# Moving 48 checks of the adjacency matrix from layers 2 and 3 of a graph network into the pair loop of layer 1

## The chip, the cores and the metric

The kernel runs on one core of a Trainium2 chip. The metric is device time in microseconds (us), from the start to the end of the program on that core. A core has five engines that run side by side, each with its own queue of instructions: TensorE (PE in the profile; its weight loads are PEld), VectorE (DVE), ScalarE (ACT), GpSimd (POOL) and SyncE (SP). In this kernel SP only issues transfers (DMAs); POOL issues a few too.

## What is computed

Four graph layers in a row, on 4096 nodes with 64 features each, with one and the same 4096 x 4096 adjacency matrix `adj` (about 0.8% of its entries are 1, the diagonal is all 1). Each layer is applied to `h = max(layernorm(x), 0)` and its result is added to `x`:

```python
# layer 0: graph attention, 8 heads and an output head, softmax over the edges
# layer 1: hyperbolic attention
adj_att = sigmoid(left[:, None] + right[None, :] + b_att) * adj
support_t = einsum('ij,ijd->id', adj_att, logmap(h_i, h_j))
out1 = proj(expmap(h, support_t))
# layer 2: mean over the neighbours
deg = clip(sum(adj, axis=1) + 1, 1, None)
z = concat([h, (adj @ h + h) / deg]) @ W + b
out2 = relu(z) / max(norm(relu(z)), 1e-12)
# layer 3: the last 100 edges of a row, with halving weights
rank = cumsum(adj != 0, axis=1); k = min(rank[:, -1:], 100)
w = (adj != 0) * where(pos > 0, 0.5 ** (k - pos), 0)     # pos = rank - (deg - k)
out3 = w @ (h @ weight) + bias
```

The fast path of the kernel stores edges as bytes and so is right only if every entry of `adj` is 0 or 1. The kernel therefore reads the whole matrix once more as floats and counts other values. If any is found, a slow general kernel is run after it. On the given inputs none is found.

## The kernel before, in words

**The check.** `count_odd` (line 951) is one check. It loads one tile `raw` of 128 x 2048 floats (1 MB, two buffers) through SP's queue and runs one VectorE instruction over it (line 955), which also sums into a column of `bad`. The matrix has 64 such tiles; the iterator `todo` (line 959) hands them out. Sixteen are done in layer 0's output attention (line 2107), the other 48 in layers 2 and 3.

**Layer 1, the pairs** (`pairs_fast`, from line 2230). The nodes are cut into 8 groups of 512, and a job is a pair of groups (gi, gj), gj <= gi: 36 jobs, 8 of them diagonal. The loop from line 2396 on is a software pipeline over n = -2 to 36. In one step n it works on four jobs: `done` (n-1), `now` (n), `soon` (n+1) and `later` (n+2), in four parts s = 0 to 3:

- `load_edges(later)`: one or two tiles `nm` of 256 KB by SP, four buffers.
- `score_pair(soon)` in each part: PE, then ACT (tile `sg`, line 2284).
- s = 0: `bring(done)`, which adds PE's sums `accj` to VT on DVE (lines 2382 to 2384).
- s = 0 and 2: `turn(now)`: PE transposes and two DVE multiplications (line 2332); not for diagonal jobs.
- s = 1 and 3: `sums(now)`, the large matmuls (line 2339).
- `distance(later)` in each part (PE, ACT) and `square(later)` in s = 1 and 3 (ACT; tile `sqy`, three buffers).
- s = 1: `factor(soon)`, two DVE instructions (line 2313); s = 3: `weigh(soon)`, two more (line 2320).

The loop stands in `with in_order()`: PE, ACT and DVE each keep exactly the written order. SP is not held by it. Outside such blocks a planner (list scheduler) orders each engine's instructions when the kernel is built.

**The finish of layer 1** (`finish_steps`, line 2429; `nodes`, line 2562) turns VT into new node values, a quarter of the nodes at a time, in a long chain of small DVE instructions with ACT between, and ends in the tile `HH` (in the profile `XAf`), which layer 2's matmuls read.

**Layer 2** (lines 2668 to 2719): for each half hf of the columns, PE multiplies `HH` with the edge bytes `m` (line 2679) in 8 steps q, and with `sel` for the degrees (line 2692). Then four groups go through `layer2_group`, a chain over PE, ACT and DVE that ends in the values `SS` for layer 3. In a step q with `hf or q > NQ // 2` a check is issued: 3 in the first half, 8 in the second. `issue_after` keeps them behind the finish.

**Layer 3** (lines 2724 to 2792): four units u of 1024 columns. For each of 32 blocks j: PE counts edges into `pv` (lines 2748, 2756), ACT turns counts into weights (line 2765), PE adds up (`sacc`, line 2730). The edges `m` come in 8 loads of 512 KB per unit (line 2741), with three buffers. Checks stand beside the blocks: 12 in u = 0, 9 in u = 1, 8 each in u = 2 and 3. All are tied by `issue_after(valued[-1])` to the last `layer2_group`'s values (line 2664), so none runs before that.

Of the kernel before, what the change touches and what calls it, by code (L numbers as in the profile page):

```python
# [18 lines left out]
ALU = mybir.AluOpType  # L19
# [7 lines left out]
NB = N // P  # L27
# [808 lines left out]
def kernel(  # L836
# [1392 lines left out]
    def pairs_fast(es, VT):  # L2229
# [19 lines left out]
        with ExitStack() as ss:  # L2249
# [129 lines left out]
            def bring(gi, gj):  # L2379
# [6 lines left out]
                for way in ways(gi, gj):  # L2386
                    del sig[way], edges[way]

            def job(n):
                return jobs[n] if 0 <= n < len(jobs) else None  # L2390

            load_edges(*jobs[0])
            with in_order():
                for n in range(-2, len(jobs) + 1):
                    done, now, soon, later = (job(n + k) for k in range(-1, 3))
                    if later and n + 2 > 0:
                        load_edges(*later)
                    for s in range(4):
                        if soon and s // 2 < len(ways(*soon)):
                            score_pair(*ways(*soon)[s // 2], s % 2 * 2)  # L2400
                        if s == 0 and done:
                            last_column(*done, 2)
                            bring(*done)
                        if s % 2 == 0 and now and now[0] != now[1]:
                            turn(*now, s)
                        if s % 2 and now:
                            sums(*now, s - 1)
                        if s == 2 and now:
                            last_column(*now, 0)
                        if later:  # L2410
                            distance(*later, s)
                            if s % 2:
                                square(*later, s - 1)
                        if s == 1 and soon:
                            factor(*soon)
                        if s == 3 and soon:
                            weigh(*soon)

    def finish_steps(bs, VQ, VT, fold_v, pabs, f, f2, kp, pf, ac2, wide, ps):

# [91 lines left out]
    def layers_fast(es, wide, *sums):  # L2512
# [41 lines left out]
            base=0,  # L2554
            channel_multiplier=1,
        )
        ready, valued = [], []

# [24 lines left out]
        def not_before_nodes():  # L2585
            return tc.issue_after(ready[-1].ins)
# [32 lines left out]
        def layer2_group(b0, part, deg):  # L2619

            bs = slice(b0, b0 + GB)
            hg = h[:, bs, :]
            pn = ps.tile([P, GB, D], F32, name="pnf", tag="misc")
            for b in range(GB):
                nc.tensor.matmul(
                    pn[:, b, :], lhsT=part[:, b * P : (b + 1) * P], rhs=fold_h, start=True, stop=True
                )
            cat = work.tile([P, GB, 2 * D], F32, name="cat", tag="cat")
            nc.gpsimd.tensor_copy(cat[:, :, 0:D], hg)
            nc.vector.scalar_tensor_tensor(cat[:, :, D:], pn, 1.0 / VALH, hg, ALU.mult, ALU.add)  # L2630
            nc.vector.tensor_tensor(cat[:, :, D:], cat[:, :, D:], over(deg, D), ALU.mult)
            cT = work.tile([P, G], F32, name="cT", tag="cT")
            transpose_to(cT, [cat[:, b, :] for b in range(GB)], P, ps, nc.scalar.copy)
            pz = ps.tile([P, GB, D], F32, name="pz", tag="misc")
            for b in range(GB):
                nc.tensor.matmul(
                    pz[:, b, :], lhsT=cT[:, b * P : (b + 1) * P], rhs=w2, start=True, stop=True
                )
            zt = work.tile([P, GB, D], F32, name="zt", tag="zt")
            nc.vector.tensor_tensor(zt, pz, b2t.unsqueeze(1).to_broadcast([P, GB, D]), ALU.add)  # L2640
            nc.scalar.activation(zt, zt, AF.Relu)
            sq = work.tile([P, GB, D], F32, name="sq2", tag="sq2")
            nc.scalar.activation(sq, zt, AF.Square)
            nrm = small("nrm", GB)
            nc.vector.tensor_reduce(nrm, sq, AX.X, ALU.add)
            nc.vector.tensor_scalar(nrm, nrm, 1e-24, None, ALU.max)
            nc.scalar.activation(nrm, nrm, AF.Sqrt)
            nc.vector.reciprocal(nrm, nrm)
            nc.vector.tensor_tensor(zt, zt, over(nrm, D), ALU.mult)
            xg = x[:, bs, :]  # L2650
            nc.vector.tensor_tensor(xg, xg, zt, ALU.add)

            for _ in norm_steps(bs, work, "sq2"):
                pass
            hT = work.tile([D, G], F32, name="hT3", tag="hT3")
            transpose_to(hT, [h[:, b, :] for b in range(b0, b0 + GB)], D, ps, nc.scalar.copy)
            pu = ps.tile([P, GB, D], F32, name="psup", tag="misc")
            for b in range(GB):
                nc.tensor.matmul(
                    pu[:, b, :], lhsT=hT[:, b * P : (b + 1) * P], rhs=w3, start=True, stop=True  # L2660
                )
            nc.scalar.copy(SS[:, bs, 0, :], pu)
            lo = work.tile([P, GB, D], F32, name="lo3", tag="lo3")
            valued.append(nc.vector.tensor_tensor(lo, pu, SS[:, bs, 0, :], ALU.subtract))
            nc.scalar.activation(SS[:, bs, 1, :], lo, AF.Copy, scale=LO)


        with tc.tile_pool(name="ps_nacc", bufs=6, space=PSUM) as ps_acc:
            for hf in range(2):
                accs = [ps_acc.tile([P, G], F32, name="nacc", tag="nacc") for _ in range(NS)]  # L2670
                dc = ps_acc.tile([P, G], F32, name="dc", tag="nacc")
                for q in range(NQ):
                    m = work.tile([P, JT, HW], U8, name="m2", tag="m2", bufs=3)
                    nc.sync.dma_start(m, mask_d[q][hf])
                    m8 = m.bitcast(F8)
                    for t in range(JT):
                        j = q * JT + t
                        for k in range(NS):
                            nc.tensor.matmul(  # L2679
                                accs[k],  # L2680
                                lhsT=HH[:, j].rearrange("p s d -> p (s d)"),
                                rhs=m8[:, t, k * G : (k + 1) * G],
                                start=(j == 0),
                                stop=(j == NB - 1),
                            )
                    if hf or q > NQ // 2:
                        with not_before_nodes():
                            count_odd(work, next(todo))
                    for t in range(JT):
                        j = q * JT + t  # L2690
                        for k in range(NS):
                            nc.tensor.matmul(
                                dc[k * O : (k + 1) * O, :],
                                lhsT=sel[:, j * O : (j + 1) * O],
                                rhs=m8[:, t, k * G : (k + 1) * G],
                                start=(j == 0),
                                stop=(j == NB - 1),
                            )
# [25 lines left out]
        for u in range(4):  # L2724
# [14 lines left out]
            for q in range(NQ):  # L2739
                m = work.tile([P, JT, HO2], U8, name="m3", tag="m3", bufs=3)  # L2740
                nc.sync.dma_start(m, mask_d[q][u // 2][:, :, hs])
                for t in range(JT):
                    j = q * JT + t

                    pv = ps_v.tile([P, HO2], F32, name="pv", tag="pv")
                    for k in range(NK):
                        r = ((u % 2) * NK + k) * O
                        nc.tensor.matmul(
                            pv[:, k * G : (k + 1) * G],
                            lhsT=blk[r : r + O, j, :],  # L2750
                            rhs=late[r : r + O, u // 2, :],
                            start=True,
                            stop=False,
                        )
                    for k in range(NK):
                        nc.tensor.matmul(  # L2756
                            pv[:, k * G : (k + 1) * G],
                            lhsT=tri,
                            rhs=m[:, t, k * G : (k + 1) * G].bitcast(F8),
                            start=False,  # L2760
                            stop=True,
                        )

                    w = work.tile([P, HO2], I16, name="w3b", tag="w3b", bufs=3)
                    nc.scalar.activation(w, pv, AF.Relu)  # L2765
                    if (j % 4 == 1 or j == 31 and u == 1) if u else j % 5 and j > NB // 2:
                        with tc.issue_after(valued[-1].ins):
                            count_odd(work, next(todo))
                    if last is not None:
                        add_up(*last)  # L2770
                    last = (j, w)
# [113 lines left out]
```

## Time and profile before

| | us |
|---|---|
| median of 3 runs | 2073.34 (2065.35 to 2073.9) |
| profiled execution, its own time | 2079.71 |
| its span, first to last instruction | 2077.9 |

| engine | busy us | share of the span | instructions |
|---|---|---|---|
| PE | 1830.8 | 88% | 19323 |
| PEld | 825.1 | 40% | 19340 |
| DVE | 1533.3 | 74% | 2239 |
| ACT | 1476.6 | 71% | 1439 |
| POOL | 86.0 | 4% | 125 |

Stages in the trace, in us from the start of the span: layer 0 to about 1200, the setting up of layer 1 to 1222, its pairs to about 1675, its finish beside the first matmuls of layer 2 to about 1747, layer 2 to about 1829, layer 3 (u = 0 beside the last groups of layer 2) to 2067, and the last outputs to 2078.

How to read the lines: a group's line gives source line, engine, operation, tile written <- tiles read, shape and count; then busy us in all and mean ns of one; then the engine's idle time before them and what ended it. In a timeline a line begins with the start and the length in us, and brackets hold the idle time just before. A line of waits has the total, the number and the longest wait. Matmul lengths are modelled. Shares of the whole span mix stages with different limits, so a stage's own stretch is what counts.

### The profile page before, as it was taken

The page shows a single profiled execution, that of the slowest core. Times are in us where ns is not written, and L with a number is a line of the kernel's source. Part 1 is how long each engine was busy: PE and PEld are TensorE (multiplying, and loading weights), DVE is VectorE, ACT ScalarE, POOL GpSimd, SP SyncE. Part 2 cuts the span into 40 slices and gives each one's busy share as a digit, 9 for nine tenths or more (in the row PEclk, how much of TensorE's full clock was granted, in tenths as well). Part 3 has the DMA queues.
Part 4 walks back from the last instruction along what each step waited for, and adds up shares of the span by engine and source line. Part 5 has one row for each costly group of instructions (what it writes and reads, how often), then busy time and mean ns, then how long its engine had stood idle before and what let it go on. Part 6 is the DMA issues. An engine that isn't in the chain of part 4 may idle for free.

```text
span 2077.9 us, 44185 instructions
## 1 busy us (share of the span) xinstructions
PE 1830.8 (88%) x19323; PEld 825.1 (40%) x19340; DVE 1533.3 (74%) x2239; ACT 1476.6 (71%) x1439; POOL 86.0 (4%) x125
## 2 busy tenths in 40 slices
PE   5889989999999999994898959999999968799777
PEld 3444444444444444442343523333333333443222
DVE  5779988998689889996889756656555687625554
ACT  3778988899689879984778757777777732257446
POOL 2000100100000000001011000000000000000000
PEclk8899999999999999996999959999999978979889
DMA  9946645345011101004875311111111045715885
GB/s 111 179 112 99 100 89 97 133 159 190 21 48 68 44 30 73 33 2 164 314 246 200 112 37 31 37 46 36 41 41 36 26 164 187 269 41 192 291 315 185
DMA packets 117015, 239.04 MB, mean 115 GB/s; under 512 B 11062, under 2 KB 84006, under 8 KB 102054
## 3 DMA queue, kind: packets, MB, share of 16 engines
q1 hardware_dynamic: 101996, 192.95, 27.0%
q0 software_dynamic: 14816, 43.18, 11.6%
q8 instruction: 153, 2.51, 0.5%
q14 instruction: 50, 0.41, 0.1%
HBM read 245.37 MB, written 49.46 MB: 142 GB/s over the span
## 4 chain that ended last, share of the span: by engine, by line
PE 34%; DVE 11%; issue 7%; ACT 5%; DMA 5%; POOL 0%; SPq 0%; POOLq 0%; DVEq 0%; ACTq 0%
PE accj L2339 9%; PE acco L2132 3%; PE pf L2329 2%; PE pl L2273 2%; DMA mo<-edges 2%; DMA raw<-in_adj_dram 2%; PE pu L2293 2%; PE accC L1541 2%; PE pl L2279 2%; DVE raw L955 2%; PE pu L2294 1%; PE accB L1541 1%; PE nacc L2679 1%; DVE B L1211 1%; PE pv L2756 1%
## 5 line engine op out<-in xcount | busy, mean ns | idle before, releaser
L1205 ACT ACTIVATE st<-srow,nt 128x2048 int8<-128x2048 f32 x352 | 682.8, 1994 | 78.2 <-DVE B L1211 77.3
L1211 DVE TENSOR_TENSOR B<-st,mres 128x1024 int32<-128x1024 int32 x256 | 312.0, 1221 | 69.5 <-PE accC L1541 44.5
L1541 PE MATMUL accB<-B,ybh 128*32 128x512 fp8e4 x3072 | 340.0, 385 | 13.3 <-DVE B L1211 13.3
L1541 PE MATMUL accD<-B,ybh 128*32 128x512 fp8e4 x2048 | 303.2, 388 | 23.6 <-DVE h L1657 23.6
L1541 PEld LDWEIGHTS <-ybh 128*32 128x32 bf16 (+1 forms) x6656 | 198.3, 98 | 236.4 <-issue 75.6
L1541 PE MATMUL accC<-mres,ych 128*32 128x512 fp8e4 x2272 | 268.3, 380 | 0.0
L1541 PE MATMUL accC<-B,ycn 128*32 128x512 fp8e4 x2272 | 268.1, 380 | 0.0
L1541 PE MATMUL accL<-B,ybh 128*32 128x512 fp8e4 x1536 | 221.4, 391 | 4.6 <-DVE h L1661 4.5
L1541 PEld LDWEIGHTS <-ych 128*32 128x32 f16 x4096 | 170.2, 99 | 114.8 <-issue 10.2
L1199 DVE TENSOR_SCALAR st<-srow,nt 128x2048 uint8<-128x2048 f32 x160 | 205.6, 1285 | 2.5
L2339 PE MATMUL accj<-sg,who 128*64 128x512 f32 (+1 forms) x512 | 198.0, 616 | 4.4 <-DVE sg L2332 4.4
L2339 PE MATMUL acci<-sg,who 128*64 128x512 f32 (+1 forms) x512 | 198.0, 616 | 0.0
L955 DVE SCALAR_TENSOR_TENSOR raw<-raw 128x2048 f32<-128x2048 f32 x64 | 146.3, 2288 | 67.8 <-DMA raw<-in_adj_dram 67.5
L2765 ACT ACTIVATE w3b<-pv 128x1024 int16<-128x1024 f32 x128 | 130.0, 1023 | 83.0 <-PE pv L2756 82.0
L2284 ACT ACTIVATE sg<-pl,rb 128x512 f32<-128x512 f32 x256 | 160.9, 679 | 9.3 <-PE pl L2279 6.3
L2295 ACT ACTIVATE yt<-pu,consts 128x512 f32<-128x512 f32 x144 | 98.7, 687 | 96.5 <-PE pu L2294 96.4
L1205 ACT ACTIVATE st<-srowo,nto 128x1024 int8<-128x1024 f32 x128 | 138.4, 1138 | 26.6 <-DVE B L1211 26.4
L1541 PE MATMUL accC<-C,ych 128*32 128x512 fp8e4 x1824 | 148.4, 391 | 0.8 <-DVE C L1219 0.8
L1219 DVE TENSOR_TENSOR C<-B,mres 128x1024 int32<-128x1024 int32 x114 | 139.6, 1225 | 3.6
L1541 PEld LDWEIGHTS <-ycn 128*32 128x32 f16 x2272 | 108.3, 97 | 62.0 <-issue 1.4
L2332 DVE SCALAR_TENSOR_TENSOR sg<-pf,sg 128x512 f32<-128x512 f32 x112 | 72.1, 686 | 37.2 <-PE pf L2329 37.0
L2132 PE MATMUL acco<-B,YBo 128*128 128x512 fp8e4 x256 | 70.5, 396 | 29.7 <-DVE B L1211 29.1
(497 smaller groups left out, 2707.2 us busy)
## 6 DMA issues: line engine op xcount, KB each, us to landing
raw<-in_adj_dram SPq DMA_DIRECT2D x64, 1024.0 KB, 7.3
mo<-edges SPq DMA_DIRECT2D x32, 512.0 KB, 4.6
noedge<-nmo POOLq DMA_DIRECT2D x32, 512.0 KB, 4.1
nm<-noedge SPq DMA_DIRECT2D x64, 256.0 KB, 3.0
m<-edges SPq DMA_DIRECT2D x16, 1024.0 KB, 6.9
m<-edges SPq DMA_DIRECT2D x32, 512.0 KB, 6.3
srow<-srow_d SPq DMA_DIRECT2D x15, 1024.0 KB, 6.7
mres<-in_adj_dram POOLq DMA_DIRECT2D x8, 1024.0 KB, 35.8
```

Of the source, the lines that this page charges most:

```text
L955: nc.vector.scalar_tensor_tensor(raw, raw, 0.0, raw, ALU.is_gt, ALU.not_equal, accum_out=bad[:, c : c + 1])
L1199: nc.vector.tensor_scalar(st[:, i, :].bitcast(U8), srow, negs[:, i : i + 1], EDGE, ALU.is_gt, ALU.mult)
L1205: nc.scalar.activation(st[:, i, :], srow, AF.Sign, bias=negs[:, i : i + 1], scale=-1.0)
L1211: nc.vector.tensor_tensor(B.bitcast(I32), st.bitcast(I32), edges.bitcast(I32), ALU.bitwise_and)
L1219: nc.vector.tensor_tensor(C.bitcast(I32), B.bitcast(I32), edges.bitcast(I32), ALU.bitwise_xor)
L1541: ins = nc.tensor.matmul(acc[k * O : (k + 1) * O, :], lhsT=values, rhs=moving(k), start=start, stop=stop,)
L2132: sums = nc.tensor.matmul(acc[k], lhsT=Y[:, i].rearrange("p s d -> p (s d)"), rhs=E[:, i, k * G : (k + 1) * G], start=j0 + i == 0, stop=ac ...
L2284: nc.scalar.activation(sg[:, b0 + k, :], pl, AF.Sigmoid, bias=rb[:, j : j + 1], scale=1.0)
L2295: nc.scalar.activation(far[gi, gj][:, b, :], pu, AF.Sigmoid, bias=nb_t, scale=2.0 * DIST_K / (DIST_S * DIST_S),)
L2332: nc.vector.scalar_tensor_tensor(v[:, t, :], pf, F_K3, v[:, t, :], ALU.add, ALU.mult)
L2339: nc.tensor.matmul(acc[r : r + n, :], lhsT=XQ[:, src, cols], rhs=w, start=start, stop=stop)
L2765: nc.scalar.activation(w, pv, AF.Relu)
```

## The change

All checks outside layer 0 are issued in the pair loop. A helper takes the next one from `todo`. In a step n >= 0 one check is issued at s = 2, one more at s = 0 if `now` is diagonal (or, in the last step, absent), and two at the end of step n = -1: 37 + 9 + 2 = 48. They fall inside `in_order`, so DVE runs them exactly there; the tile `raw` with its two buffers lies in the pairs' pool. Layers 2 and 3 lose their checks and the `issue_after` ties, and `valued` goes.

```diff
+            def check_edges():
+                c = next(todo, None)
+                if c is not None:
+                    count_odd(work, c)
...
                         if s == 1 and soon:
                             factor(*soon)
+                        if n >= 0 and (s == 2 or s == 0 and (not now or now[0] == now[1])):
+                            check_edges()
                         if s == 3 and soon:
                             weigh(*soon)
+                            for _ in range(2 if n < 0 else 0):
+                                check_edges()
...
-        ready, valued = [], []
+        ready = []
...
-            valued.append(nc.vector.tensor_tensor(lo, pu, SS[:, bs, 0, :], ALU.subtract))
+            nc.vector.tensor_tensor(lo, pu, SS[:, bs, 0, :], ALU.subtract)
...
-                    if hf or q > NQ // 2:
-                        with not_before_nodes():
-                            count_odd(work, next(todo))
...
-                    if (j % 4 == 1 or j == 31 and u == 1) if u else j % 5 and j > NB // 2:
-                        with tc.issue_after(valued[-1].ins):
-                            count_odd(work, next(todo))
```

## The prediction

> **What bounds the kernel now.** I read the page first, then one stretch at a time: windows, waits, timelines of DVE, SP, PE. The page has the price of a check:
>
> ```profile
> L955 DVE SCALAR_TENSOR_TENSOR raw<-raw 128x2048 f32<-128x2048 f32 x64 | 146.3, 2288 | 67.8 <-DMA raw<-in_adj_dram 67.5
> raw<-in_adj_dram SPq DMA_DIRECT2D x64, 1024.0 KB, 7.3
> ```
>
> A check holds DVE for 2.29 us (2.2 us from start to start when two follow each other) and SP's queue for one issue, whose load lands 7.3 us later (5.0 to 15.2). DVE was found waiting for such loads for 67 us.
>
> Layer 3, windows cut at the last `sacc` matmul of each unit, so u = 1, 2, 3:
>
> ```profile
> core 0: us, PE busy (x) PEld busy (x) DVE busy (x) ACT busy (x) POOL busy (x), PEclk, DMA share, GB/s
> 1896.30:1950.50 54.20, 47.61 (x202) 15.18 (x204) 29.03 (x29) 32.35 (x33) 1.57 (x2) 0.91 0.87 307
> 1950.50:2022.40 71.90, 54.70 (x207) 17.13 (x210) 38.64 (x37) 32.65 (x34) 1.50 (x2) 0.83 0.86 303
> 2022.40:2066.70 44.30, 42.78 (x202) 14.44 (x204) 20.81 (x23) 33.28 (x34) 1.86 (x3) 1.00 0.63 230
> ```
>
> The same work takes 54.2, 71.9 and 44.3 us. The last is PE's own pace: 32 blocks at 1.29 us from one to the next make 41.3, plus the change of unit. The other two lose to the edge loads. SP's waits (u = 1 and 2), then SP's and PE's timelines around one stall:
>
> ```profile
> SPq L954 <- DVE raw L955: 93.3, 27, 6.5
> ...
> 1966.12 5.42 SPq L954 DMA_DIRECT2D raw<-in_adj_dram  x2
> 1971.63 0.52 SPq L2741 DMA_DIRECT2D m<-edges  x1
> ...
> 1970.15 1.67 PE L2756 MATMUL pv<-m,tri 128*128 128x512 fp8e4 x4 [3.01 <-DMA m<-edges]
> ```
>
> A `raw` load waits until DVE has used its buffer; the next load of `m` stands behind it in SP's queue, and PE starves for it. Why two `raw` per `m` here: the ties hold u = 0's 12 checks back until 1893, and the backlog lasts into u = 2.
>
> The pairs, DVE, one job that isn't diagonal:
>
> ```profile
> 1508.26 0.69 DVE L2384 TENSOR_TENSOR VT<-VT,accj 128x512 f32<-128x512 f32 x1 [3.35 <-PE accj L2339]
> 1508.90 1.29 DVE L2332 SCALAR_TENSOR_TENSOR sg<-pf,sg 128x512 f32<-128x512 f32 x2
> 1510.11 2.35 DVE L2313 SCALAR_TENSOR_TENSOR yt<-sqy,yt 128x1024 f32<-128x1024 f32 x2
> 1514.21 1.29 DVE L2332 SCALAR_TENSOR_TENSOR sg<-pf,sg 128x512 f32<-128x512 f32 x2 [1.75 <-PE pf L2329]
> 1515.41 2.35 DVE L2320 SCALAR_TENSOR_TENSOR sg<-yt,sg 128x1024 f32<-128x1024 f32 x2
> 1521.11 0.69 DVE L2384 TENSOR_TENSOR VT<-VT,accj 128x512 f32<-128x512 f32 x1 [3.35 <-PE accj L2339]
> ```
>
> A period of 12.85 us, set by PE (busy 419 of 438 us from 1222 to 1660). DVE idles 3.35 us before VT, just behind the place where the new check goes. In the finish it is the other way round:
>
> ```profile
> 1669.70:1747.30 77.60, 48.39 (x309) 23.79 (x310) 62.18 (x194) 25.14 (x41) 5.00 (x10) 0.77 0.49 171
> ```
>
> DVE is busy 62 of 78 us, in one chain; PE waits for its product.
>
> **What the Trainium skill says.** "DMA: Bandwidth & Descriptors", section "Anatomy of one DMA — SWDGE (gpsimd) path": a DMA's semaphore wait happens on the issuing sequencer, before dispatch; so loads behind it wait too. The 93.3 us above agree. "Perfetto Trace Analysis", section "Tensor Engine Instruction (MATMUL, LD_WEIGHTS)": ACT and DVE are strict FIFO; so a check whose tile is late holds what stands behind it. The 67 us agree. "TensorE: Matmul & The Clock Gate", section "What's actually happening": PE falls to half clock when idle. The granted 0.83 in u = 2 against 1.00 in u = 3 agrees: a stall costs twice.
>
> **The change, part by part**, against the profiled execution's 2079.7 us.
>
> 1. Layer 3 loses its 37 checks, with 37 `raw` loads on SP. What SP then issues is `m` alone, and PE should keep u = 3's pace (u = 3 still has checks and `raw` loads, and keeps it): (54.2 - 44.3) + (71.9 - 44.3) = 9.9 + 27.6 = **-37.5**. What hides nothing here: PE is the next limit, ACT with 33 us a unit is not. Bounds: -33 (half a stall stays at each change of unit) to -39.
>
> 2. Layer 2 loses 11 checks. PE's matmuls aren't the limit there; the four group chains of the first half, from 1757 to 1825, are. By the DVE timeline, checks standing in the way cost: first group 1.2 (line 2645 at 1764.81, its input ready by 1763.6) + 2.2 (line 986, at 1771.76 instead of 1769.5); second 1.2 + 2.1; third 1.7 (line 982 behind a check from 1801.60 to 1803.8); fourth 2.2 (line 2631 behind one from 1809.28). Sum 10.6. Checks beside waits for PE cost nothing. The group's PE steps stand between bursts of matmuls, in an order that the planner makes anew, so some is given back: I take **-9**, bounds -3 and -12. Layer 3 starts that much earlier.
>
> 3. Pairs, 28 jobs off the diagonal: +2.3 of DVE at s = 2 (2.29 and 0.08 for the sum's read, partly overlapping), against 3.35 idle. Behind the check stands `weigh`, needed a step later, then VT with 1.0 to spare. Where the next job is diagonal, VT has 2.59 idle: 0.2 to spare. Cost **0**. If the cover were gone, each us is paid 28 times. The load: SP issues it right after the second `nm` of two jobs ahead, 4 us before the step's VT; the check's place is 7 us after VT. 11 us against 7.3, in a stage where DMA is busy 14%. The loads of `nm` stand behind it, but SP finds the buffer free (the check two back is done), and `nm` is wanted a step later. Bounds: 0 and +20 (late by 0.7 beyond the spare, each time).
>
> 4. The 8 diagonal steps: 12.2 us from VT to VT (1482.53 to 1494.74), DVE idle 7.0 of them, and two checks take 4.6. The first tile is issued in the step before. `factor` is late by 2.3; `square` in s = 3, at about 1493, waits for it until 1487: covered. **0**. The start is not: the first two checks end about 1236.5; the third tile can only be loaded into the first's buffer, 1234.2 + 7.3 = 1241.5; check, `factor`, the fourth tile's check, `weigh` end at 1251.0, where before VT came at 1248.65: **+2.4**, bounds 0 and +6.
>
> 5. The end: n = 34 to 36 have five checks with no distances beside them. In n = 34 the idle before VT is 0.76; the other four stand beside the finish. It is a DVE chain with gaps of at most 1.9, and PE waits for it three times (20.4 us, 16.8 of them before the first quarter's matmul). 5 x 2.2 = **+11**. Their loads: two buffers, so a load follows the check two before it, and the last two can't land before about 1680 and 1686. If the planner has put finish steps ahead of them, nothing is added; if not, DVE waits. POOL's loads of weights are in another queue. The `m` loads of layer 2 may stand behind the last `raw` on SP; first wanted at 1697. Bounds: +4 (gaps take them) and +25 (two or three waits of 5 to 7).
>
> Sum: -37.5 - 9 + 0 + 2.4 + 11 = -33.1. The profiled 2079.7 would be 2046.6; on the median of the runs, 2073.34, it is **2040**.
>
> **The rivals.**
>
> A. The finish hides more and layer 2 gives all: -39 - 11 + 0 + 5 = -45: **2028**. For it: gaps of 1.3 to 1.9 in the chain, and four checks can sit in four gaps. Against: a check is longer than each gap.
>
> B. The last five checks wait for their tiles, in front of the finish: step 5 is +25, the rest as forecast: **2054**. For it: buffers force each load behind a check, and 1 MB takes 7.3. Against: the finish is outside `in_order`, so the planner may go round.
>
> C. Slower: the tile comes late in every job, and DVE's order becomes the bound of the pairs. With spare 1.0, a tile 2.2 late past its slot costs 1.2 x 28 = 33 and cancels all; 2.6 late gives +45.6 - 33: **2086**. It decides at about 13.2 us from issue to landing. For it: `raw` took up to 15.2. Against: that was beside heavy traffic; in layer 0's output attention DVE waited for `raw` once in 16, 0.9 us.
>
> D. The gain of step 1 isn't there, since u = 1 and 2 would be held by their own `m` loads: -9 + 13.4 and some 8 of step 1's 37.5: **2070**. Against: 4 MB a unit in 44 us are far below the 307 GB/s moved there.
>
> **How the numbers follow.** Forecast 0.62 (alone 2030 to 2050), A 0.13, B 0.15, C 0.05, D 0.05. The likeliest gives 2040. To hold 8 in 10: below, A and some spread of the runs, 2025; above, most of B, 2058. Half a per cent (10.4 us, about what a measurement of this kernel can tell from no change) is 2063: faster 0.90, same 0.05, slower 0.05.
>
> **What would show it.** u = 1, 2 and 3 at 44 us each, no wait of PE for `m`, SP's waits for `raw` gone there (1); the first half's groups closer than 17 us apart (2); in the pairs a period still of 12.85 with 1 us before VT, and no DVE wait for `raw` (3, 4); VT at 1251 in the first diagonal step (4); five checks after 1665 and the first matmul of layer 2 that had waited until 1697 at about 1708 (5). Wrong if the period of the pairs grows, if the finish is late by 20 and more, or if the units of layer 3 stay uneven.

## The result and the profile after

The changed kernel takes 2041.3 us (median of 4 runs, 2038.26 to 2044.93); the kernel before, run beside it, 2073.62 (2065.35 to 2075.58). The ratio is 0.9852, with a 95% interval of 0.982 to 0.9885. Forecast: 2040, range 2025 to 2058, faster. Of the profiled executions, before took 2079.71 and after 2039.13: 40.6 less. In a second set of runs the same changed kernel stood at 2038.64 (2032.01 to 2048.11, 6 runs) against 2074.97, ratio 0.9819 (0.9797 to 0.9841). Single runs of one kernel scatter by up to some 10 us to either side, so that a median within 1.3 us of the forecast is partly luck; the lengths of the stages are the better test.

Of the profile page of the changed kernel, the group of the check and the load of its tile:

```profile
L955 DVE SCALAR_TENSOR_TENSOR raw<-raw 128x2048 f32<-128x2048 f32 x64 | 146.1, 2282 | 3.3 <-DMA raw<-in_adj_dram 3.3
raw<-in_adj_dram SPq DMA_DIRECT2D x64, 1024.0 KB, 6.0
```

The same 64 checks and loads are there, at the same price. What DVE waits for tiles fell from 67.5 us to 3.3 in the whole run, and a load lands in 6.0 us instead of 7.3.

Windows of the changed kernel, with the finish of layer 1 and its matmuls of layer 2 first, then the units u = 1, 2 and 3 of layer 3, cut at the last `sacc` matmul of each (stretch and length, then the busy us of each engine, PE's granted clock, the DMA's share and rate):

```profile
core 0: us, PE busy (x) PEld busy (x) DVE busy (x) ACT busy (x) POOL busy (x), PEclk, DMA share, GB/s
1670.99:1765.80 94.81, 56.71 (x331) 28.79 (x331) 74.37 (x217) 25.34 (x42) 5.22 (x11) 0.75 0.44 154
1894.90:1938.40 43.50, 42.87 (x202) 14.42 (x204) 2.18 (x5) 31.86 (x32) 1.55 (x2) 0.99 0.29 91
1938.40:1982.50 44.10, 43.48 (x205) 14.73 (x209) 2.21 (x5) 33.26 (x33) 1.50 (x2) 1.00 0.33 101
1982.50:2026.80 44.30, 42.97 (x203) 14.55 (x206) 2.21 (x5) 33.26 (x33) 1.49 (x2) 1.00 0.25 78
```

All three units run at PE's pace, with 78 to 101 GB/s instead of up to 307. SP's waits in layer 3 of the changed kernel say the same:

```profile
SPq L2747 <- PE pv L2762: 110.8, 21, 13.5
```

SP now stands still because PE has not yet used an earlier `m`: the loads run ahead of PE. Before, it waited for DVE, and PE waited for `m`.

The pairs, in DVE's timeline of the changed kernel, a job that isn't diagonal with one that isn't behind it:

```profile
1508.11 0.69 DVE L2384 TENSOR_TENSOR VT<-VT,accj 128x512 f32<-128x512 f32 x1 [1.13 <-PE accj L2339]
1508.75 1.29 DVE L2332 SCALAR_TENSOR_TENSOR sg<-pf,sg 128x512 f32<-128x512 f32 x2
1509.96 2.35 DVE L2313 SCALAR_TENSOR_TENSOR yt<-sqy,yt 128x1024 f32<-128x1024 f32 x2
1514.06 1.29 DVE L2332 SCALAR_TENSOR_TENSOR sg<-pf,sg 128x512 f32<-128x512 f32 x2 [1.75 <-PE pf L2329]
1515.26 2.28 DVE L955 SCALAR_TENSOR_TENSOR raw<-raw 128x2048 f32<-128x2048 f32 x1
1517.47 0.08 DVE L955 DVE_READ_ACCUMULATOR raw<-raw 128x1 f32 x1
1517.47 2.35 DVE L2320 SCALAR_TENSOR_TENSOR sg<-yt,sg 128x1024 f32<-128x1024 f32 x2
1520.96 0.69 DVE L2384 TENSOR_TENSOR VT<-VT,accj 128x512 f32<-128x512 f32 x1 [1.13 <-PE accj L2339]
```

The period is still 12.85 us; 1.13 us is left before VT, and the check waits for nothing. The end of the pairs is less kind (DVE's timeline of the changed kernel, the last five checks):

```profile
1666.51 2.28 DVE L955 SCALAR_TENSOR_TENSOR raw<-raw 128x2048 f32<-128x2048 f32 x1
...
1671.59 2.28 DVE L955 SCALAR_TENSOR_TENSOR raw<-raw 128x2048 f32<-128x2048 f32 x1
...
1674.04 2.29 DVE L955 SCALAR_TENSOR_TENSOR raw<-raw 128x2048 f32<-128x2048 f32 x1 [0.16 <-DMA raw<-in_adj_dram]
...
1679.08 2.29 DVE L955 SCALAR_TENSOR_TENSOR raw<-raw 128x2048 f32<-128x2048 f32 x1
...
1682.62 2.28 DVE L955 SCALAR_TENSOR_TENSOR raw<-raw 128x2048 f32<-128x2048 f32 x1
...
1706.33 0.69 DVE L2578 SCALAR_TENSOR_TENSOR hs<-h,XAf 128x512 f32<-128x512 f32 x1 [0.69 <-ACT XAf L2575]
```

The first stands in step 34, the other four around the last column of VT and among the finish's own short operations, with one wait of 0.16 us for a tile. The first quarter's `hs` (line 2578), which ends the chain that layer 2 waits for, comes at 1706.33; before, it came at 1695.57.

The bill, each mark counted from the first pair step of its own profile, so that layers ahead of it drop out (ACT's own copies mark the ends of halves and units; us):

| up to | before | after | this stage | after, second profile |
|---|---|---|---|---|
| last column of VT, its first copy | 450.3 | 453.5 | +3.2 | 449.2 |
| first quarter of the finish | 472.1 | 484.2 | +8.9 | 480.4 |
| layer 2, first half summed | 530.9 | 542.9 | -0.1 | 540.1 |
| layer 2, second half summed | 586.2 | 594.3 | -3.9 | 591.5 |
| layer 3, u = 0 | 672.2 | 671.5 | -8.8 | 674.9 |
| layer 3, u = 3 | 842.3 | 803.9 | -37.7 | 808.2 |
| the end | 853.7 | 814.2 | -1.1 | 819.1 |

From the first pair to the end the profiles differ by 39.5, in the second profile by 34.6. The two profiles of one kernel differ by 3.8 up to the first quarter and by 6.2, the other way, in u = 0, where layer 2's last groups and the first unit share PE; u = 1 to 3 are equal to 1 us.

The difference up to VT isn't due to the checks, which both profiles have. In the twelve profiles of this study that have no extra passes of DVE in the pairs, a diagonal job's addition to VT comes either about 12.15 or about 13.7 us after the one before it; two or four of the six such jobs between the first and the last are long. PE's granted clock was 1.00 in the short ones that were read and 0.87 or 0.88 in the long ones (before: 1408.54 to 1420.70 and 1482.53 to 1496.16). What decides between the two is open. From the first addition to the 34th, the last one ahead of the five checks of the end, before took 410.8 us, the kernel without any of the 48 checks 411.0, and the changed kernel 412.6 and 407.7. From that 34th addition to the first quarter ten profiles without checks at the end took 35.35 to 35.45 us, and the two of the changed kernel 46.3 and 46.8. So the last five checks delay the first quarter by 10.9 and 11.4 us.

### The profile page after: what moved, and what is told of

The parts are those of the page before. It is cut to its first block, busy times and chain, and to the rows that moved or that the text cites. A ratio compares the mean times of both kernels' runs of the same rounds, so it can differ in the third digit from the quotient of the medians.

```text
span 2037.1 us, 44155 instructions
## 1 busy us (share of the span) xinstructions
PE 1815.8 (89%) x19323; PEld 821.8 (40%) x19340; DVE 1530.0 (75%) x2239; ACT 1476.9 (72%) x1439; POOL 83.3 (4%) x125
```

## The experiments

The first group asks where the gain comes from, with the kernel before as the base. Its own layer-3 checks are taken away, all 37 or only the 12 of u = 0 (each kernel sets `bad` to zero first, and so skips that part of the test for values other than 0 and 1).

**Layer 3 without its checks.**

```diff
-                        with tc.issue_after(valued[-1].ins):
-                            count_odd(work, next(todo))
+                        next(todo)
```

> The kernel before, with layer 3's 37 checks left out (the other 27 stay, those of layer 2 too). Theory: units u = 1, 2 and 3 of layer 3 take 44 us each, no wait of PE for m, 36 to 39 us less than the kernel before (about 2036). Rival (the units were held by their own m loads): u = 2 stays above 60 and the gain is under 10.

Measured: 2040.73 us (2035.75 to 2041.93, 4 runs) against 2072.15; ratio 0.9837 (0.9797 to 0.9878), 31.4 less, with an interval of about 25 to 42. That is short of the 36 to 39 expected, which the interval holds. Units 1 to 3 took 43.4, 44.0 and 44.3, 38 us less than before: in the profile the stage is worth what step 1 said.

**Only u = 0 without its checks**, the backlog; the other 25 stay:

```diff
-                        with tc.issue_after(valued[-1].ins):
-                            count_odd(work, next(todo))
+                        if u == 0:
+                            next(todo)
+                        else:
+                            with tc.issue_after(valued[-1].ins):
+                                count_odd(work, next(todo))
```

> The kernel before, with only the 12 checks of u = 0 left out; the 25 of u = 1 to 3 stay, at one raw load for each load of m. Theory (the backlog of u = 0 makes two raw loads per m, and that is what starves PE): units at 44 to 46 us, 33 to 38 us less than before, although two thirds of the checks and of their bytes are still there. Rival (each check in layer 3 costs its share): 12/37 of 37.5, about 12 us less.

Measured: 2042.86 (2034.77 to 2045.19, 4 runs), ratio 0.9833 (0.9788 to 0.9877): as much as all 37. Its windows over u = 1, 2, 3:

```profile
1895.60:1939.30 43.70, 43.16 (x203) 14.64 (x206) 23.85 (x24) 32.32 (x33) 1.56 (x2) 1.00 0.91 321
1939.30:1983.30 44.00, 43.40 (x205) 14.64 (x208) 22.97 (x25) 33.26 (x33) 1.50 (x2) 1.00 0.91 326
1983.30:2032.90 49.60, 45.50 (x202) 15.63 (x204) 13.81 (x17) 33.25 (x33) 1.86 (x3) 0.93 0.46 155
```

Two units with 19 tiles between them run at PE's pace at 321 and 326 GB/s. So a tile per `m` or so does no harm; twelve more in the same stretch do. In u = 3 one stall is left, at 1984 to 1990: PE waits 2.4 for `ev` and is then slow to restart.

**Layer 2 without its 11 checks**:

```diff
-                        with not_before_nodes():
-                            count_odd(work, next(todo))
+                        next(todo)
```

> The kernel before, with layer 2's 11 checks left out; layer 3 keeps its 37. Theory: the groups of the first half follow each other at about 14 us instead of 18, layer 3 starts 10 to 12 us earlier, and the whole is 9 to 12 us less. Rival (the planner's new order of PE gives it back): 0 to 4 us less.

Measured: 2059.44 (2052.01 to 2071.74, 13 runs), ratio 0.9946 (0.9923 to 0.9969), 12.7 less. Units 1 to 3 stay uneven (51.1, 68.1, 44.0), so most of the other gain is still to be had there. By the medians the two gains add up: 31.4 and 12.7 make 44.1, and without any of the 48 checks (below) it is 45.9.

**The loads of layer 3 on another queue.** Step 1 said that `m` stands behind a waiting `raw` in SP's queue. Then it should be enough to issue `raw` from POOL, every check staying where it is (`count_odd` gets a parameter for the queue):

```diff
-                            count_odd(work, next(todo))
+                            count_odd(work, next(todo), nc.gpsimd)
```

> The kernel before, with layer 3's 37 raw loads issued from POOL's queue instead of SP's; all checks are done, all bytes are moved, and the backlog of u = 0 stays. Theory (the m loads stand behind raw loads that wait in SP's queue): units at 44 to 47 us, 30 to 38 us less than before. Rival (bandwidth: 307 GB/s of raw and m together is what the units wait for): u = 2 stays above 60, under 10 us less.

Measured: 2076.12 (2067.02 to 2085.68, 12 runs), ratio 1.0016 (0.9992 to 1.0039). The expectation failed: nothing was gained. Its waits over layer 3:

```profile
POOL raw L954 <- DVE raw L955: 179.7, 35, 44.6
DVE raw L955 <- DMA raw<-in_adj_dram: 76.9, 32, 4.7
...
PE pn L2780 <- DVE ev L2775: 26.3, 3, 11.4
```

PE waits for no `m` any more. It waits for `ev`, the copy of the sums at the end of a unit, half of which is DVE's; the copy stands behind checks whose tiles are late. Units 1 to 3 took 43.8, 60.3 and 56.3, and the last check ended at 2061.8, when PE's last unit was already done. The stall has moved from SP's queue to DVE's.

**The same, with `ev` copied by ACT alone**:

```diff
-                (nc.vector.tensor_copy if k % 2 else nc.scalar.copy)(ev[:, k, :], accs[k])
+                nc.scalar.copy(ev[:, k, :], accs[k])
```

> The kernel before with layer 3's 37 loads of raw on POOL's queue, two buffers, and the copies of the sums at the end of a unit (ev) all on ACT, where half of them stood on DVE behind late checks. If the copies behind checks are what stalled PE in that form, units 1 to 3 take 44 to 46 us each, PE is done by about 2025, and the end comes from the last check (2062 there) and the stores behind it: 2062 to 2070. If PE is held by the flow of bytes itself, the units stay at 160 us together and the time at 2076.

Measured: 2072.87 (2064.75 to 2081.74, 20 runs), ratio 1.0006 (0.9992 to 1.002): 3 us above the range of the first theory. The windows over u = 1, 2, 3 and what follows, and DVE's last check:

```profile
1894.60:1938.70 44.10, 43.88 (x207) 14.56 (x206) 21.31 (x22) 32.73 (x35) 6.37 (x12) 1.00 0.88 307
1938.70:1982.70 44.00, 43.90 (x209) 14.64 (x208) 22.14 (x22) 33.76 (x35) 6.23 (x11) 1.00 0.89 307
1982.70:2026.90 44.20, 43.38 (x206) 14.44 (x204) 24.25 (x23) 33.73 (x34) 6.34 (x12) 1.00 0.88 307
2026.90:2058.70 31.80, 2.18 (x17) 1.86 (x16) 18.49 (x18) 1.07 (x2) 3.70 (x7) 0.55 0.71 251
```

```profile
2056.40 2.29 DVE L955 SCALAR_TENSOR_TENSOR raw<-raw 128x2048 f32<-128x2048 f32 x1 [1.28 <-DMA raw<-in_adj_dram]
```

Now PE is wholly freed, 44 us a unit and done at 2027, as in the changed kernel. And the time is that of the kernel before: the checks go on to 2058.7, and the last outputs follow them on POOL. It is the stream of tiles itself that takes until then, at 307 GB/s for as long as both streams run and at 251 when only the tiles are left.

**The same as the first, with four buffers for `raw`**, since two in flight might be what limits the stream:

```diff
-        raw = pool.tile([P, HW], F32, name="raw", tag="raw", bufs=2)
+        raw = pool.tile([P, HW], F32, name="raw", tag="raw", bufs=bufs)
...
-                            count_odd(work, next(todo), nc.gpsimd)
+                            count_odd(work, next(todo), nc.gpsimd, 4)
...
-                m = work.tile([P, JT, HO2], U8, name="m3", tag="m3", bufs=3)
+                m = work.tile([P, JT, HW], U8, name="m2", tag="m2", bufs=3)
+                m = m.rearrange("p j (a h) -> p (j a) h", a=2)[:, 0:JT]
```

(Layer 2's checks get the four buffers too.)

> The kernel before with layer 3's 37 loads of raw on POOL's queue, and four buffers for raw instead of two (m of layer 3 takes the buffers of layer 2's m, for the room). With two buffers this gained nothing. Theory of bytes: from the release at 1893 on, 37 tiles and 24 loads of m, about 51 MB, have to come in, and the cores' DMA moved 304 GB/s there: 168 us, whatever queue or buffers; then DVE goes on waiting for raw, units 1 to 3 stay above 160 us together and the time is 2065 to 2080. Theory of buffers: two tiles in flight and a check between are what sets the stream of tiles, so that with four the flow rises well over 304 GB/s, the checks are done by about 2025 and the units take 44 us each: 2045 or less.

Measured: 2095.29 (2090.44 to 2099.51, 5 runs), ratio 1.0093 (1.006 to 1.0127): 15 us above the range that the theory of bytes gave, and far from the other. Its waits of PE over layer 3, and its windows over u = 1 and 2:

```profile
PE pv L2757 <- DMA m<-edges: 22.4, 6, 5.4
```

```profile
1901.80:1973.80 72.00, 54.15 (x208) 16.90 (x206) 42.01 (x41) 32.29 (x34) 10.59 (x20) 0.81 0.83 318
1973.80:2035.90 62.10, 49.76 (x209) 15.67 (x208) 34.04 (x33) 33.23 (x33) 8.92 (x16) 0.86 0.80 308
```

Twice the tiles in flight move 308 to 318 GB/s, not more. The last check ends at 2051, 11 us sooner than with two buffers, but at the cost of `m`: PE starves for it again, with no queue shared (and waits 7.3 us for `ev`, half of which DVE copies here). So buffers weren't the limit while both streams run; what the tiles gain `m` loses. Four buffers together with `ev` on ACT alone were not run.

The second group takes the changed kernel apart; its first four kernels, of which the first is the changed kernel's second set, share the same 2074.97 of before.

**The changed kernel again**, unaltered, as their base:

> The changed kernel once more, as the measure for the three beside it: 30 to 35 us less than the kernel before, about 2041.

Measured: 2038.64, ratio 0.9819, as given above.

**None of the 48 checks** (layer 0's 16 remain, the others are left out; `bad` is set to zero first, here and in the next):

```diff
-                if c is not None:
-                    count_odd(work, c)
+                pass
```

> The changed kernel with all 48 checks left out. Theory: what the checks still cost in the changed kernel is about 12 us, nearly all of it at the end of the pairs and in the finish; 2029. Rival (the pairs pay too, each check slows its job): 20 us and more less than the changed kernel, and a shorter period than 12.85 us.

Measured: 2029.06 (2023.14 to 2031.99, 5 runs), ratio 0.9767 (0.9749 to 0.9785). By the medians all 48 cost 9.6 us where they now stand.

**Without the last five**, those of n = 34 to 36 (43 of the 48 are done):

```diff
-                            check_edges()
+                            if n < 34:
+                                check_edges()
+                            else:
+                                next(todo)
```

> The changed kernel with only the last five checks (steps 34 to 36) left out. Theory: 11 us less than the changed kernel (2030), the finish's first result at about 1695 again, within 2 us of the kernel without any of the 48. Rival (gaps in the finish's chain took part of them): 4 to 6 us less.

Measured: 2029.64 (2027.71 to 2035.19, 5 runs), ratio 0.9787 (0.977 to 0.9805). By the medians the five are worth 9.0, practically the whole cost of the 48, and the other 43 cost 0.6, which these runs can't tell from nothing. The 9.0 is not sharp, since the changed kernel's six runs range over 16 us and the two intervals overlap; the first quarter, which without the five comes about 11 us sooner after the 34th addition, is.

**The last five in layer 3**, written beside blocks of u = 1 and 2, where the flow has room; all checks are done:

```diff
-                            check_edges()
+                            if n < 34:
+                                check_edges()
...
-        ready = []
+        ready, valued = [], []
...
-            nc.vector.tensor_tensor(lo, pu, SS[:, bs, 0, :], ALU.subtract)
+            valued.append(nc.vector.tensor_tensor(lo, pu, SS[:, bs, 0, :], ALU.subtract))
...
                     nc.scalar.activation(w, pv, AF.Relu)
+                    if j in ((), (5, 13, 21), (5, 13), ())[u]:
+                        with tc.issue_after(valued[-1].ins):
+                            count_odd(work, next(todo))
```

> The changed kernel with the last five checks moved to layer 3, units 1 and 2, eight blocks apart; every check is done. Theory: layer 3 takes a few checks at no cost as long as no raw load waits in front of an m load: 11 us less than the changed kernel, about 2030, units at 44 us. Rival (any raw load there costs): 3 to 10 us come back, 2033 to 2040.

Measured: 2030.74 (2023.43 to 2033.74, 5 runs), ratio 0.9783 (0.9765 to 0.9802). The planner did not spread them as written: DVE runs all five between 1874.0 and 1894.5, two at the end of u = 0 and three at the start of u = 1. They come free there, as far as these runs can tell: 1.1 us more than without them, and u = 1 to 3 took 44.5, 44.0 and 44.0. This does all that the reference asks, and is 7.9 us below the changed kernel's median of the same runs, though the two intervals still touch at 0.9797 to 0.9802. It is the best version of this study.

**The spare of the pairs**, measured by a pass of DVE over a tile of its own, behind the check in the 27 steps before n = 34 that aren't diagonal:

```diff
+            def once_more(n):
+                if 0 <= n < 34 and jobs[n][0] != jobs[n][1]:
+                    nc.vector.tensor_tensor(spare, spare, spare, ALU.max)
...
                             check_edges()
+                            once_more(n if s == 2 else -1)
```

> The changed kernel with one more VectorE instruction of about 2.2 us (a maximum over an own 128 x 2048 tile, no load) behind the check in each of the 27 steps before 34 that aren't diagonal. Theory (1.13 us to spare before VT, 0.38 where the next job is diagonal, and beyond that DVE sets the period): 27 x 2.2 - 21 x 1.1 - 6 x 0.4 = 34 us more than the changed kernel, about 2075, period 13.9. Rival (DVE's order isn't what PE waits for): under 8 us more.

Measured: 2049.46 (2047.25 to 2053.62, 4 runs) against 2070.6, ratio 0.9879 (0.9845 to 0.9913). The expectation failed: against before this is 21 us less, where the changed kernel had 32 to 36 less, so the passes cost 11 to 15. DVE's timeline:

```profile
1513.19 0.68 DVE L2386 TENSOR_TENSOR VT<-VT,accj 128x512 f32<-128x512 f32 x1
1513.79 1.28 DVE L2334 SCALAR_TENSOR_TENSOR sg<-pf,sg 128x512 f32<-128x512 f32 x2
1514.98 2.35 DVE L2315 SCALAR_TENSOR_TENSOR yt<-sqy,yt 128x1024 f32<-128x1024 f32 x2
1518.38 1.29 DVE L2334 SCALAR_TENSOR_TENSOR sg<-pf,sg 128x512 f32<-128x512 f32 x2 [1.05 <-PE pf L2331]
...
1521.79 2.29 DVE L2398 TENSOR_TENSOR spare<-spare 128x2048 f32<-128x2048 f32 x1
...
1526.27 0.68 DVE L2386 TENSOR_TENSOR VT<-VT,accj 128x512 f32<-128x512 f32 x1
```

Of the 2.2 us that are added, 1.13 goes into the idle before VT, 0.7 into the idle before the second `sg` product (1.75 before, 1.05 here), and the period grows by 0.23 to 13.08. Next to a diagonal job there is less room: the period just before one grows from 11.19 to 12.17 and just after one from 12.10 to 13.09, and the diagonal step gives about 1.1 of these 2.0 back (11.1 or 12.5 instead of 12.15 or 13.7). VT's first and last addition lie 8.0 and 12.8 us further apart than in the two profiles of the changed kernel.

**Two such passes**:

```diff
                     nc.vector.tensor_tensor(spare, spare, spare, ALU.max)
+                    nc.vector.tensor_tensor(spare, spare, spare, ALU.max)
```

> The changed kernel with two extra passes of DVE (2.2 us each) behind the check in 27 steps that aren't diagonal; one cost about 10 us, with the period at 13.08 instead of 12.85. Theory that the spare is now used up and each further us is paid in every job: period about 15.3, 27 x 2.2 = 59 more than with one, about 2108. Theory that there is more slack in PE's order (1.04 us idle before the second turn is still there): period 14.2, about 2080.

Measured: 2154.29 (2153.0 to 2156.47, 4 runs) against 2072.63, ratio 1.0381 (1.0342 to 1.042): 82 us slower than before, and some 103 more than with one pass. Neither number was large enough. VT's period in the timeline of DVE, and PE's timeline behind its wait:

```profile
1516.01 0.68 DVE L2386 TENSOR_TENSOR VT<-VT,accj 128x512 f32<-128x512 f32 x1
...
1522.85 1.29 DVE L2334 SCALAR_TENSOR_TENSOR sg<-pf,sg 128x512 f32<-128x512 f32 x2 [2.70 <-PE pf L2331]
...
1533.06 0.68 DVE L2386 TENSOR_TENSOR VT<-VT,accj 128x512 f32<-128x512 f32 x1
```

```profile
1517.34 1.00 PE L2341 MATMUL accj<-sg,who 128*64 128x512 f32 x1 [2.49 <-DVE sg L2334]
1517.35 1.01 PE L2341 MATMUL acci<-sg,who 128*64 128x512 f32 x1
...
1525.95 0.59 PE L2341 MATMUL accj<-sg,who 128*64 128x512 f32 x1
```

A period of 17.05, 4 us more for 2.2 us of work; most periods between jobs that aren't diagonal are of this length, some 15.4. PE waits 2.49 us for DVE, and the matmuls right behind that wait take 1.0 us where the same shape later takes 0.59; DVE then waits 2.7 for PE. The windows over this period and over one of the changed kernel:

```profile
1516.61:1533.66 17.05, 14.56 (x72) 4.88 (x72) 14.32 (x14) 9.89 (x14) 0.00 (x0) 0.90 0.31 95
1508.75:1521.60 12.85, 12.85 (x75) 4.67 (x73) 9.97 (x13) 9.89 (x16) 0.00 (x0) 1.00 0.40 133
```

The granted clock was 0.90 against 1.00, and PE was busy 14.56 us instead of 12.85: 1.7 us lost to slower matmuls on top of 2.49 of waiting. That PE is slow after standing still is also what "TensorE: Matmul & The Clock Gate" in the Trainium skill says under "What's actually happening". It names an idle window of about 3.4 us; here waits of 2.49 us were enough.

## Why the prediction was right, and where it wasn't

**Step 1: the size right, the reason only in part.** Forecast -37.5, profile -37.7; leaving the checks out gives the same units. That the twelve checks of u = 0 make the difference is shown by the run without them. But the carrier that step 1 named, `m` behind a waiting `raw` on SP, is only where the shortage came out. Three forms that take SP out of it gained nothing, each with another last wait: `ev` on DVE, the end of the checks, or `m` itself. What they share is the sum of bytes. The checks are released near 1892. In the form freed of both waits 35 tiles of 1.049 MB and 21 loads of `m` of 0.524 MB are issued from then on, 47.7 MB; two tiles and three of the 24 loads were in already, which the expectation of the run with four buffers (51 MB) overlooked. PE's own need for u = 1 to 3 is 132 us, in which 307 GB/s bring 40.5 MB: those loads of `m` and some 28 tiles; at 326, the highest rate of these windows, some 30. The 25 of the run without the twelve fit, 37 don't. At 307 GB/s throughout, the 47.7 MB take 155 us, until 2047; the last check of that form ended at 2058.7, since the tiles alone came at 251 GB/s. With four buffers it ended at 2051.

Step 1's windows showed 307 and 303 GB/s in two stretches of different length; they were read as traffic beside the stall, and were close to the limit, since no form moved more than 326 over a unit. "A stall costs twice" was a little high: u = 2 took 27.6 us more than u = 3, of which by those windows 15.7 are PE idle and 11.9 PE busy for longer, 1.8 us for each us idle. The arithmetic of bytes over rate was left out of the prediction, except for the 4 MB a unit of `m` alone in rival D. The Trainium skill has a rate for it: "DMA: Bandwidth & Descriptors", "Specifications", gives about 358 GB/s as a core's limit from HBM, half of what two cores share. As an estimate from that page, 47.7 MB take 133 us, just PE's 132, so that the page alone would not have decided it; the runs show less, 303 to 326 GB/s. The move works because it carries 38.8 MB into a stage with room: from 1250 to 1650 the DMA moved 38 GB/s before and 138 after.

The chance that SP's order adds something of its own to the kernel before isn't excluded; the runs show only that without it the time is the same.

**Step 2: -9 forecast.** The profile has -3.9 in layer 2's halves and -8.8 to the end of u = 0, 12.7 in all; the second profile of the changed kernel gives -5.6 (from the first quarter to the end of u = 0 it takes 194.5, before 200.1), and the run without layer 2's checks 12.7. The first half's groups, which were to come closer than 17 us apart, begin (DVE's first instruction of each, `cat`) at 1768.20, 1782.30, 1795.97 and 1809.85, and the second half's first at 1828.94: 60.7 us for the four, where before it was 71.9. The 12.7 lie just outside the bound of -12, the 5.6 inside the bounds; u = 0 alone scatters by 6 us, so the size of this term is known no better than that.

**Step 3: 0, confirmed.** Period 12.85, spare 1.13, or 0.38 where the next job is diagonal; 43 checks together cost 0.6. What was wrong is the price beside it: "each us is paid 28 times" past a spare of 1.0. The first extra pass found another 0.7 of slack and cost 0.23 in a job between others that aren't diagonal, about 1.0 in a job next to a diagonal one; the second cost 4 us for 2.2. Between jobs that aren't diagonal the edge lies near 2 us past the check, and the slope behind it near 1.8.

**Step 4: 0 for the diagonal steps, +2.4 for the start.** The first diagonal step's VT came at 1246.74 with no wait, against the 1251 that was to show this step, and against the first pair it was 0.6 earlier than before; the second VT was 1.0 later. In the second profile both came when they did before, to 0.1 us. DVE did wait for two tiles at the start, 0.62 and 2.15 us, but the third tile landed in some 5.2 us, not in the 7.3 that was measured beside layer 3's traffic. The term was 1.4 to 2.4 too large.

**Step 5: +11 forecast.** Counted from the 34th addition to VT, which the pairs' scatter doesn't reach, the profiles give +10.9 and +11.4; leaving the five out gives 9.0 back by the medians. Waits for tiles, which would have made it rival B, came to 0.16 us: the last two tiles, put at 1680 and 1686, were in by 1679.1 and 1682.6.

**The rivals.** A (2028) and B fell with step 5. C fell because tiles land in 4.9 to 10.2 us and 13.2 was needed; by the spare measured since, it would have needed later still, and would then have cost more (its 45.6 for 28 times 1.6 should be 44.8, which changes nothing). D fell since the units do take 44 us; the rate did bind there, but for `m` and the tiles together.

Summed over the profile's own stages, the forecast's -33.1 stands against -39.5 and -34.6 in two profiles and against -32.3 and -36.3 in the medians.

## What to carry to other kernels

Where loads wait and an engine starves, first divide the bytes that still have to come by the rate that the window shows: if that is more than the engine itself needs for the stage, look for a stage with room to move bytes to; here another queue, another engine's copies and more buffers each gained nothing. A wait names where a shortage comes out, and taking that wait away moves it to the next queue; so test a mechanism by removing its carrier, not only its cause. And work put into idle time is free up to an edge that must be measured, not read from one gap: here it lay, away from the diagonal jobs, at nearly twice the gap beside it, and beyond it each us cost nearly two.

## What the runs showed of the hardware that was not expected

While both streams run, the rate hardly depends on how it is asked for: 307 GB/s with two tiles in flight from one queue and `m` from another, 308 to 318 with four, 303 to 326 over a unit with all on one queue. A PE that waits 2.49 us in each 17 us loses another 1.7 to slower matmuls, 1.0 us instead of 0.59, though its mean granted clock reads 0.90. And diagonal steps with the same work took 12.15 us at a granted clock of 1.00 or 13.7 at 0.87, both within one run: most of the scatter in the pairs is that.
